# The sums of S: stored from SyncE's queue, one pair of slabs later, and no transfer on GpSimd's queue

## The chip, the cores and the metric

The kernel runs on one core of a Trainium2 chip. The metric is the device time of one execution in microseconds; lower is better. The times before are three executions of the same program. One further execution was profiled, and the profile page and all answers of the trace come from that one.

## The reference

Two layers of graph convolution on `x` of shape (8, 2048, 64), with one adjacency matrix `adj` of 2048 x 2048. Cut to what matters:

```python
# layer 0: each node has its own weights, mixed from 16 by an embedding
w = einsum('nd,dkio->nkio', embedding, weight)          # K = 3
A_stack = stack([I, A, 2*A@A - I])
x_g = einsum('knm,bmc->bnkc', A_stack, x)
x = layernorm(x + einsum('bnki,nkio->bno', x_g, w) + embedding @ bias)
# layer 1: diffusion convolution with the same matrix as both supports
x1 = A @ x0;  x2 = 2*A@x1 - x0
x = layernorm(x + concat([x0, x1, x2, x1, x2]) @ weight + bias)
```

So there are four multiplications by A: two hops in layer 0, two in layer 1. A is symmetric in its places of non-zero entries, and every row holds one value; the kernel uses A = diag(r) S, where S has ones and zeros, and checks this as it goes. Where it doesn't hold, a second, general program runs instead (a branch at the end of the first).

## The kernel before

**Stages.** The first hop (`hop_x`) multiplies S by x directly, in two passes g = 0 and 1, each over 16 slabs of A. The second hop uses seven products in place of eight (`seven_products`), which needs sums and differences of the quarters of S. Then comes layer 0's mix with the node weights (`mix0`), the third hop by seven products again, and the last hop directly.

**The first hop, where the change lies.** A step is one slab: k = kk + 8 j, for kk from 0 to 7 and j = 0, 1, so that two steps form a pair. A step loads 512 KB of A (`load_slab`, line 188) and, in pass 0, 256 KB of x. VectorE turns the slab into S (`places`, L200), ScalarE and VectorE split x into a high and a low half (L211, L215), and TensorE multiplies, 16 matmuls of 128x512 a step (L231). Once the second slab of a pair is there, `put_together` (lines 406 to 414) makes four sums or differences of quarters of S on VectorE (L413, four instructions), in bfloat16, into a piece of the buffer `z2` that is not in use yet, and stores the 512 KB into the DRAM tile `sums_of` (L414). ScalarE makes a bfloat16 copy of each slab and stores it too, 256 KB a pair, into `quarters` (L467). The seven products read both back through SyncE's queue (`load_sum`).

**What sets the order.** `run` (line 242) walks over the steps and calls each part of a step a given number of steps ahead: `operands`, with the loads and `put_together`, two steps before `use`, which holds the matmuls. `load` (line 117) and `ordered` keep the instructions of an engine in the order in which the code names them, so SyncE's queue issues its transfers in that order: for a step x, then the slab, then whatever `loads` still holds. Slabs go into a ring of five buffers (`RAW`), S into a ring of four.

**The join with the first product.** The steps of the first of the seven products follow in the same `run`; it uses slabs of A again (`slab`, 512 KB each, eight of them), and each of its `operands` also takes one of the waiting constants off `loads` (512 KB each for `w`, 1 MB for `rrow`). Because SyncE's queue may run ahead of the engines, these transfers are issued while the first hop still runs.

**GpSimd's queue** carries only the sixteen stores of L414. In the general program, which isn't run for these inputs, it carries the loads of constants and the sixteen stores of the result.

Of the kernel before, what the change touches and what calls it, by code (L numbers as in the profile page):

```python
# [18 lines left out]
B, N, C = 8, 2048, 64  # L19
NT = N // P  # L20
D = 16
# [16 lines left out]
def pattern(  # L38
# [22 lines left out]
    nc = tc.nc  # L61
# [46 lines left out]
    emb_sb = pack_sb[:, : NT * D].rearrange("p (t d) -> p t d", d=D)  # L108
    bias1 = pack_sb[:, NT * D :]
# [3 lines left out]
    w = [const.tile([P, D, C], F32, tag=f"w{k}", name=f"w{k}") for k in range(3)]  # L113
# [8 lines left out]
    def ordered(ins):  # L122
        if in_order:
            tc.keep_in_program_order(ins)
# [63 lines left out]
    def load_slab(src, shape):  # L188
        raw = rawp.tile(shape, F32, tag="raw", name="raw")
        load(nc.sync, raw, src)  # L190
        return raw
# [18 lines left out]
    def high(src, to):  # L210
        ordered(nc.scalar.copy(to[0], src))  # L211

    def low(src, to):

        ordered(nc.vector.tensor_tensor(to[1], src, to[0], ALU.subtract))  # L215
# [184 lines left out]
    sums_of = scratch.tile([KK, 2, P, 4, Q], BF16, tag="sums", name="sums_of")  # L400
    S1, S2, S4, S3 = range(4)

    quarters = scratch.tile([KK, P, 2, 2, Q], BF16, tag="quarters", name="quarters")
    couple = []

    def put_together(g, kk, x0, x1):
        to = z2[:, 2 * (kk % 8) : 2 * (kk % 8) + 2, :].rearrange("p t n -> p (t n)").bitcast(BF16)
        to = to.rearrange("p (i n) -> p i n", i=4)
        for i, (a, b, op) in enumerate((
            (x0[:, 1], x1[:, 1], ALU.add), (to[:, S1], x0[:, 0], ALU.subtract),  # L410
            (x1[:, 0], to[:, S2], ALU.subtract), (x0[:, 0], x0[:, 1], ALU.subtract),
        )):
            ordered(nc.vector.tensor_tensor(to[:, i], a, b, op))  # L413
        ordered(nc.gpsimd.dma_start(out=sums_of[kk, g], in_=to))  # L414

    def hop_x(g, kk, j):
        k = kk + KK * j

        def features(got):
            if g == 0 and k == 0:  # L420
                got["raws"] = [load_slab(adj[h, 0, :, :Q], [P, Q]) for h in range(2)]

        def operands(got):
            if g == 0 and k == 0:

                s = got["s"] = spool.tile([P, 2, Q], F32R, tag="s", name="s")
                hl = got["hl"] = [hpool.tile([P, B * C], F32R, tag="hl", name="hl") for _ in range(2)]
                high(z[0][0], hl)
                for h in range(2):
                    ordered(nc.vector.tensor_scalar(s[:, h], got["raws"][h], 0.0, None, ALU.not_equal))  # L430
                    if h == 0:
                        low(z[0][0], hl)
            else:
                if g == 0:
                    load(nc.sync, z[0][k], x[k].rearrange("n b c -> n (b c)"))
                raw = load_slab(adj[:, k, :, g * Q : (g + 1) * Q].rearrange("h m n -> m h n"), [P, 2, Q])
                got["s"] = places(raw)
                got["hl"] = halves(z[0][k])
                if g == 1 and len(loads) > 6:
                    load(nc.sync, *loads.pop(0))  # L440
            couple.append(got["s"])
            if j == 1:
                put_together(g, kk, *couple)
                couple.clear()

        def out(i):
            t = 4 * g + i if i < 4 else 4 * g + i + 4
            a, r = accs[i], rcol[:, t : t + 1]
            if i % 2:
                ordered(nc.vector.tensor_scalar_mul(z[1][t], a, r))  # L450
            else:
                ordered(nc.scalar.activation(z[1][t], a, AF.Copy, scale=r))

        def use(got):
            s, hl = got["s"], got["hl"]
            if kk == 0 and j == 0:
                accs[:] = banks(8)
            last = kk == KK - 1 and j == 1
            add_block(accs, s.rearrange("p h n -> p (h n)"), hl, kk == 0 and j == 0, last)
            if last:  # L460
                for i in range(8 if g == 0 else 4):
                    out(i)
            seen = xcpool.tile([P, 2, Q], BF16, tag="ln_xc", name="seen")
            i = g * NT + k
            ordered(nc.scalar.activation(seen, s, AF.Copy, accum_out=nonzero[:, i : i + 1]))
            if j == 1:
                ordered(nc.scalar.dma_start(out=quarters[kk, :, :, g, :], in_=seen))  # L467
            if last and g == 1:

                todo.extend(lambda i=i: out(i) for i in range(4, 8))  # L470

        return [(4, features), (2, operands), (0, use)]


# [378 lines left out]
def general(  # L853
# [10 lines left out]
    nc = tc.nc  # L864
# [16 lines left out]
    emb_sb = const.tile([P, NT, D], F32, tag="emb", name="emb_sb")  # L881
# [3 lines left out]
    w = [const.tile([P, D, C], F32, tag=f"w{k}", name=f"w{k}") for k in range(3)]  # L885

    v = const.tile([P, 3, C], F32, tag="v", name="v")
    bias1 = const.tile([P, C], F32, tag="bias1", name="bias1")

    def load_constants():  # L890
        nc.gpsimd.dma_start(out=emb_sb, in_=pack[:, : NT * D].rearrange("p (t d) -> p t d", d=D))
        b0_sb = work.tile([D, C], F32, tag="ln_xc", name="b0_sb")
        nc.gpsimd.dma_start(out=b0_sb, in_=bias[0:D, N // 4 :])
        for g in range(4):
            eT = work.tile([D, N // 4], F32, tag="acc", name=f"eT{g}")
            nc.gpsimd.dma_start(out=eT, in_=bias[32 * g : 32 * g + D, : N // 4])
            pb = ps_tp.tile([P, 4, C], F32, tag="tp", name=f"pb{g}")
            for j in range(4):
                nc.tensor.matmul(pb[:, j, :], lhsT=eT[:, j * P : (j + 1) * P], rhs=b0_sb, start=True, stop=True)
            nc.vector.tensor_copy(ebias[:, g * 4 : (g + 1) * 4, :], pb)  # L900
        for k in range(3):
            nc.gpsimd.dma_start(out=w[k].rearrange("p d o -> p (d o)"), in_=w0[k])

        wl = work.tile([P, 5, C], F32, tag="ln_sq", name="wl")
        nc.gpsimd.dma_start(
            out=wl, in_=pack[:, NT * D + C :].rearrange("p (k o) -> p k o", k=5)
        )
        w24 = work.tile([P, C], F32, tag="x2", name="w24")  # L910
        nc.vector.tensor_add(w24, wl[:, 2, :], wl[:, 4, :])
        nc.vector.tensor_sub(v[:, 0, :], wl[:, 0, :], w24)
        for h in range(2):
            q = slice(h * C, (h + 1) * C)
            nc.vector.tensor_add(v[q, 0, :], v[q, 0, :], ident[q, q])
        nc.vector.tensor_add(v[:, 1, :], wl[:, 1, :], wl[:, 3, :])
        nc.vector.tensor_scalar_mul(v[:, 2, :], w24, 2.0)
        nc.gpsimd.dma_start(out=bias1, in_=pack[:, NT * D : NT * D + C])


    blocks = {}
# [45 lines left out]
    def layernorm(src):  # L967


        def col(name):  # L970
            return work.tile([P, B], F32, tag=name, name=name)

        def wide(c):
            return c.unsqueeze(2).to_broadcast([P, B, C])

        s = col("ln_s")
        nc.vector.tensor_reduce(s, src, AX.X, ALU.add)
        nm = col("ln_nm")
        nc.vector.tensor_scalar_mul(nm, s, -1.0 / C)
        xc = work.tile([P, B, C], F32, tag="ln_xc", name="xc")  # L980
        nc.gpsimd.tensor_tensor(xc, src, wide(nm), ALU.add)
        sq = work.tile([P, B, C], F32, tag="ln_sq", name="sq")
        nc.scalar.activation(sq, xc, AF.Square)
        ss = col("ln_ss")
        nc.vector.tensor_reduce(ss, sq, AX.X, ALU.add)
        va = col("ln_v")
        nc.vector.tensor_scalar(va, ss, 1.0 / C, EPS, ALU.mult, ALU.add)
        sd = col("ln_sd")
        nc.scalar.activation(sd, va, AF.Sqrt)
        r0 = col("ln_r0")  # L990
        nc.vector.reciprocal(r0, sd)

        q = col("ln_q")
        nc.vector.tensor_mul(q, r0, r0)
        nc.vector.tensor_mul(q, q, va)
        nc.vector.tensor_scalar(q, q, -0.5, 1.5, ALU.mult, ALU.add)
        r = col("ln_r")
        nc.vector.tensor_mul(r, r0, q)
        nc.gpsimd.tensor_tensor(xc, xc, wide(r), ALU.mult)
        return xc  # L1000
# [107 lines left out]
    for i, t in enumerate(order):  # L1108
        ph = hop(t, lambda k: z[k][:, 1], ks)
        acc = work.tile([P, B, C], F32, tag="acc", name="acc")  # L1110
        nc.vector.tensor_tensor(acc, ph, z[t][:, 0], ALU.add)
        prefetch(order, i, 3)
        nc.gpsimd.dma_start(out=out[t], in_=layernorm(acc))


def gnn_kernel(tc, x, xT, adj, diag, rcols, bias, pack, w0, out):
# [55 lines left out]
```

## Time and profile before

| | |
|---|---|
| median of three runs | 828.28 us (827.91 to 828.9) |
| the profiled execution, device time | 828.66 us |
| its span, first to last instruction | 826.8 us |
| TensorE (PE) busy | 812.6 us, 98% |
| VectorE (DVE) busy | 594.7 us, 72% |
| ScalarE (ACT) busy | 275.3 us, 33% |
| GpSimd (POOL) busy | 111.9 us, 14% |
| granted TensorE clock | 0.997 |

```profile
PE   9999999999999999999999999999999999999995
DMA  9997885544200000000000001130154435565631
GB/s 329 376 386 244 287 315 174 155 143 148 69 3 12 15 13 15 14 14 14 14 14 14 30 13 38 39 103 27 43 150 152 141 128 150 167 181 165 212 120 42
```

These are three rows of the page's busy slices: the span is cut into 40 equal parts of 20.7 us, and a digit is the busy share in tenths. The first hop fills the first six slices, the seven products of the second hop the next five. The DMA engines are fullest in the first three.

```profile
q1 hardware_dynamic: 61616, 78.49, 29.5%
q10 hardware_dynamic: 6944, 8.66, 3.0%
q0 software_dynamic: 2304, 8.39, 2.8%
```

These are the DMA queues, with packets, MB and the share of sixteen engines' span: q1 is SyncE's, q10 ScalarE's and q0 GpSimd's, whose 8.39 MB are the sixteen stores of 512 KB.

```profile
raw<-in_adj SPq DMA_DIRECT2D x67, 512.0 KB, 4.7
sums_of<-z POOLq DMA_DIRECT2D x16, 512.0 KB, 6.3
quarters<-seen ACTq DMA_DIRECT2D x16, 256.0 KB, 6.2
z<-in_x SPq DMA_DIRECT2D x15, 256.0 KB, 8.1
```

These are transfers by who issues them, with their size and the median time in us from the issue to the landing.

### The profile page before, as it was taken

To read this page: it belongs to the slowest core of one execution; us is meant where nothing else is said; L and a number is where in the kernel's file an instruction comes from. 1 tells how busy PE (TensorE), PEld (TensorE's weight loads), DVE (VectorE), ACT (ScalarE), POOL (GpSimd) and SP (SyncE) were. 2 spreads that over 40 slices of the span, in tenths; PEclk is the share of its full clock that TensorE was granted. 3 is DMA by queue.
4 is the path that set the end of the run, shared out by engine and by line. 5 is a ranking of instruction groups with operands and counts; after the bars stand their busy time and mean duration, and the time that the engine had idled before them with its cause. 6 is when DMAs were issued, how large, how long until landed. Compare 5 with 4: busy or idle time off the path is not lost.

```text
span 826.8 us, 14470 instructions
## 1 busy us (share of the span) xinstructions
PE 812.6 (98%) x5614; PEld 725.2 (88%) x5614; DVE 594.7 (72%) x1303; ACT 275.3 (33%) x496; POOL 111.9 (14%) x121
## 2 busy tenths in 40 slices
PE   9999999999999999999999999999999999999995
PEld 6888888888788999999999999999878888888884
DVE  6878658763467888888888888888867546758762
ACT  5436445877401111111111101111287664203110
POOL 0000000000641111111110111111100000003341
PEclk9999999999999999999999999999999999999998
DMA  9997885544200000000000001130154435565631
GB/s 329 376 386 244 287 315 174 155 143 148 69 3 12 15 13 15 14 14 14 14 14 14 30 13 38 39 103 27 43 150 152 141 128 150 167 181 165 212 120 42
DMA packets 70940, 96.54 MB, mean 117 GB/s; under 512 B 4432, under 2 KB 45648, under 8 KB 70736
## 3 DMA queue, kind: packets, MB, share of 16 engines
q1 hardware_dynamic: 61616, 78.49, 29.5%
q10 hardware_dynamic: 6944, 8.66, 3.0%
q0 software_dynamic: 2304, 8.39, 2.8%
q8 instruction: 46, 0.75, 0.4%
q14 instruction: 30, 0.25, 0.1%
HBM read 78.75 MB, written 16.78 MB: 116 GB/s over the span
## 4 chain that ended last, share of the span: by engine, by line
PE 92%; issue 3%; DVE 3%; POOL 1%; ACT 1%; DVEq 0%; POOLq 0%; ACTq 0%
PE pm L361 36%; PE accT L558 24%; PE acc L231 14%; PE a L231 8%; PE accT L231 5%; PE pu L380 2%; DVE acc L367 2%; POOL z L609 1%; PE pt L274 1%; PE accT L662 1%; PE first L135 1%; POOL xc L322 0%; POOL got L337 0%; ACT sq L310 0%; DVE s L200 0%
## 5 line engine op out<-in xcount | busy, mean ns | idle before, releaser
L367 DVE SCALAR_TENSOR_TENSOR acc<-pm,pack_sb,acc 128x256 f32<-128x256 f32 x512 | 246.3, 483 | 41.6 <-PE pm L361 20.5
L558 PE MATMUL accT<-s,hl 128*128 128x512 f32 x896 | 205.6, 390 | 1.9 <-DVE s L200 1.4
L558 PEld LDWEIGHTS accT<-s,hl 128*128 128x128 f32 x896 | 167.6, 188 | 37.7 <-issue 1.8
L361 PE MATMUL pm<-w,xt 64*128 64x256 f32 x1024 | 160.9, 378 | 1.1 <-DVE acc L367 1.1
L361 PE MATMUL pm<-w,t 64*128 64x256 f32 x1024 | 160.0, 376 | 0.2 <-ACT t L276 0.2
L361 PE MATMUL pm<-w,z 64*128 64x256 f32 x1024 | 159.9, 376 | 0.0
L231 PE MATMUL acc<-hl,s 128*128 128x512 f32 x512 | 117.1, 390 | 0.0
L546 ACT CAST s<-raw 128x1024 fp32r<-128x1024 bf16 x96 | 101.0, 1052 | 40.2 <-ACT hl L211 32.2
L231 PEld LDWEIGHTS acc<-hl,s 128*128 128x128 f32 x512 | 95.8, 188 | 21.1 <-DVE hl L215 0.7
L361 PEld LDWEIGHTS pm<-w,t 64*128 64x128 f32 x1024 | 110.7, 187 | 1.9 <-ACT t L276 0.6
L361 PEld LDWEIGHTS pm<-w,z 64*128 64x128 f32 x1024 | 110.8, 187 | 1.4
L361 PEld LDWEIGHTS pm<-w,xt 64*128 64x128 f32 x1024 | 108.4, 187 | 2.5 <-issue 1.2
L276 ACT COPY hT<-pt 128x512 f32<-128x512 f32 x15 | 8.8, 587 | 197.4 <-PE pt L274 197.4
L231 PE MATMUL a<-hl,s 128*128 128x512 f32 x320 | 73.0, 389 | 0.0
L231 PEld LDWEIGHTS a<-hl,s 128*128 128x128 f32 x320 | 60.0, 188 | 12.5
L211 ACT CAST hl<-z 128x256 fp32r<-128x256 f32 (+1 forms) x96 | 47.1, 510 | 67.6 <-PE acc L231 36.4
L215 DVE TENSOR_TENSOR hl<-z,hl 128x512 fp32r<-128x512 f32 (+1 forms) x96 | 52.5, 552 | 21.2 <-ACT hl L211 18.4
L322 POOL TENSOR_TENSOR xc<-acc,s 128x512 f32<-128x512 f32 x16 | 16.7, 1043 | 279.5 <-DVE s L320 265.4
L200 DVE TENSOR_SCALAR s<-raw 128x1024 fp32r<-128x1024 f32 x47 | 33.2, 706 | 16.5 <-PE acc L231 10.9
L231 PE MATMUL accT<-hl,s 128*128 128x512 f32 x192 | 44.2, 390 | 0.0
L231 PEld LDWEIGHTS accT<-hl,s 128*128 128x128 f32 x192 | 35.9, 188 | 7.4
L347 POOL TENSOR_TENSOR acc<-z,ebias 128x256 f32<-128x256 f32 x32 | 22.7, 731 | 90.5 <-DVE hl L215 87.2
(105 smaller groups left out, 603.3 us busy)
## 6 DMA issues: line engine op xcount, KB each, us to landing
raw<-in_adj SPq DMA_DIRECT2D x67, 512.0 KB, 4.7
raw<-sums_of SPq DMA_DIRECT2D x64, 256.0 KB, 2.8
sums_of<-z POOLq DMA_DIRECT2D x16, 512.0 KB, 6.3
raw<-quarters SPq DMA_DIRECT2D x32, 256.0 KB, 2.6
raw<-in_adj SPq DMA_DIRECT2D x16, 384.0 KB, 3.5
quarters<-seen ACTq DMA_DIRECT2D x16, 256.0 KB, 6.2
xt<-in_xT SPq DMA_DIRECT2D x16, 256.0 KB, 2.6
out<-got ACTq DMA_DIRECT2D x16, 256.0 KB, 3.9
```

Source lines behind the costliest of these rows:

```text
L200: ordered(nc.vector.tensor_scalar(s, raw, 0.0, None, ALU.not_equal))
L211: ordered(nc.scalar.copy(to[0], src))
L215: ordered(nc.vector.tensor_tensor(to[1], src, to[0], ALU.subtract))
L231: nc.tensor.matmul(accs[i], lhsT=s[:, i * P : (i + 1) * P], rhs=hl[h], start=(first and h == 0), stop=(last and h == 1),)
L276: ordered(nc.scalar.copy(tt.rearrange("p j (h n) -> p h j n", h=2), pt[:, :, : B // 2 * C].rearrange("p h (j n) -> p h j n", n=C)))
L322: ordered(nc.gpsimd.tensor_tensor(xc, src, wide(s), ALU.subtract))
L347: nc.gpsimd.tensor_tensor(part.rearrange("p (j i) c -> p j i c", j=2), bc(0, t)[:, 4 * g : 4 * g + 4, :].rearrange("p (i j) c -> p j i c", ...
L361: nc.tensor.matmul(pm[:, j, i], lhsT=tt[k][q, 2 * g + i, :], rhs=w[k][q, ds, :], start=(k == 0), stop=(k == 2),)
L367: ordered(nc.vector.scalar_tensor_tensor(part, pm[:, :, :, d, :].rearrange("p j i c -> p (j i) c"), emb_sb[:, t, dd : dd + 1], part, ALU.m ...
L380: nc.tensor.matmul(pm[:, j, i * 3 * C : (i + 1) * 3 * C], lhsT=hT[q, 2 * g + i, :], rhs=v[q], start=True, stop=True,)
L546: ordered(nc.scalar.copy(s, got["raw"]))
L558: nc.tensor.matmul(acc[i][:, c], lhsT=hl[h][:, i * P : (i + 1) * P], rhs=S[:, c * 512 : (c + 1) * 512], start=(kk == 0 and h == 0), stop=( ...
```

## The change

The store of a pair's sums is no longer issued by GpSimd as soon as they are made. It is put on a short list, and SyncE issues it when the next pair's sums have been written down in the program, so behind the loads of that pair. The last one is issued in the last step's `use`. In the general program all transfers of GpSimd's queue go to ScalarE's.

```diff
     quarters = scratch.tile([KK, P, 2, 2, Q], BF16, tag="quarters", name="quarters")
-    couple = []
+    couple, stores = [], []
...
             ordered(nc.vector.tensor_tensor(to[:, i], a, b, op))
-        ordered(nc.gpsimd.dma_start(out=sums_of[kk, g], in_=to))
+
+        stores.append(lambda: load(nc.sync, sums_of[kk, g], to))
+        if len(stores) > 1:
+            stores.pop(0)()
...
             if last and g == 1:
+                stores.pop(0)()
...
     def load_constants():
-        nc.gpsimd.dma_start(out=emb_sb, in_=pack[:, : NT * D].rearrange("p (t d) -> p t d", d=D))
+        nc.scalar.dma_start(out=emb_sb, in_=pack[:, : NT * D].rearrange("p (t d) -> p t d", d=D))
...
         prefetch(order, i, 3)
-        nc.gpsimd.dma_start(out=out[t], in_=layernorm(acc))
+        nc.scalar.dma_start(out=out[t], in_=layernorm(acc))
```

The other transfers of `load_constants` in the general program are changed in the same way.

More of the change, by code (lines that the diff above doesn't have):

```diff
@@ L890, in load_constants @@
     def load_constants():
-        nc.gpsimd.dma_start(out=emb_sb, in_=pack[:, : NT * D].rearrange("p (t d) -> p t d", d=D))
+        nc.scalar.dma_start(out=emb_sb, in_=pack[:, : NT * D].rearrange("p (t d) -> p t d", d=D))
         b0_sb = work.tile([D, C], F32, tag="ln_xc", name="b0_sb")
-        nc.gpsimd.dma_start(out=b0_sb, in_=bias[0:D, N // 4 :])
+        nc.scalar.dma_start(out=b0_sb, in_=bias[0:D, N // 4 :])
         for g in range(4):
             eT = work.tile([D, N // 4], F32, tag="acc", name=f"eT{g}")
-            nc.gpsimd.dma_start(out=eT, in_=bias[32 * g : 32 * g + D, : N // 4])
+            nc.scalar.dma_start(out=eT, in_=bias[32 * g : 32 * g + D, : N // 4])
             pb = ps_tp.tile([P, 4, C], F32, tag="tp", name=f"pb{g}")
@@ L901, in load_constants @@
         for k in range(3):
-            nc.gpsimd.dma_start(out=w[k].rearrange("p d o -> p (d o)"), in_=w0[k])
+            nc.scalar.dma_start(out=w[k].rearrange("p d o -> p (d o)"), in_=w0[k])
         wl = work.tile([P, 5, C], F32, tag="ln_sq", name="wl")
-        nc.gpsimd.dma_start(
+        nc.scalar.dma_start(
             out=wl, in_=pack[:, NT * D + C :].rearrange("p (k o) -> p k o", k=5)
@@ L917, in load_constants @@
         nc.vector.tensor_scalar_mul(v[:, 2, :], w24, 2.0)
-        nc.gpsimd.dma_start(out=bias1, in_=pack[:, NT * D : NT * D + C])
+        nc.scalar.dma_start(out=bias1, in_=pack[:, NT * D : NT * D + C])
     blocks = {}
```

## The prediction

> **What bounds the kernel now.** I read the page first (PE busy 812.6 us of 826.8), then PE's waits over the span (two of about 1 us each in the whole middle), then a table of stretches over the two passes in which the sums of S are made and stored, because all sixteen transfers that move are issued between 12.9 and 116.0 us.
>
> ```profile
> core 0: us, PE busy (x) PEld busy (x) DVE busy (x) ACT busy (x) POOL busy (x), PEclk, DMA share, GB/s
> 0.00:20.00 20.00, 18.71 (x72) 12.79 (x73) 12.99 (x24) 10.89 (x18) 1.97 (x8) 1.00 0.92 327
> 20.00:40.00 20.00, 20.00 (x90) 16.57 (x89) 16.19 (x27) 9.22 (x17) 1.60 (x3) 1.00 1.02 374
> 40.00:60.00 20.00, 20.00 (x90) 16.55 (x89) 15.60 (x25) 8.13 (x15) 1.60 (x3) 1.00 1.04 393
> 100.00:120.00 20.00, 20.00 (x90) 16.57 (x89) 11.27 (x19) 7.49 (x15) 1.30 (x2) 1.00 0.88 298
> ```
>
> PE never stops, so there is nothing to win here from earlier or cheaper transfers. But the DMA engines are full as well (share 1.02 and 1.04, 374 and 393 GB/s), so a loss of feed can become a PE stall. The reader is to see both. PE takes 90 matmuls in 20 us, 0.222 us each; in stretches without a join it takes 37 in 8 us, 0.216 us. A step has 16, so 3.46 us, and a pair of slabs 6.9 us.
>
> Next, SyncE's waits up to 130 us. They say that it runs ahead until a raw buffer comes free or until an older transfer lands:
>
> ```profile
> SPq L118 <- DVE s L200: 60.9, 20, 8.2
> SPq L118 <- DMA raw<-in_adj: 13.0, 10, 3.6
> SPq L118 <- DMA z<-in_x: 9.4, 9, 1.8
> SPq L118 <- DMA quarters<-seen: 6.7, 3, 5.1
> ```
>
> The last row is ACT's transfer holding up SP. At 4.95 us SP issues after eight transfers of SP and ACT, just when the first of the eight has landed (ACT's cast of it starts at 4.96). I infer that SP and ACT together keep eight transfers in flight.
>
> **What the Trainium skill says.** "DMA: Bandwidth & Descriptors", section "Issuing engines are not separate DMA queues": all issuers end on the same 16 engines, and another issuer saves only issue time. The trace agrees: the share is full whatever the queue, and POOL's issue costs 0.56 us after 6.7 us of idle POOL on average (106.5 us over sixteen). Same page, "Queues, rings and completion order": an engine takes one ring in ring order and goes round robin between rings. So a store on SyncE's ring stands ahead of later loads instead of sharing with them; no run here separates the two yet. Same page, "Anatomy of one DMA — SWDGE (gpsimd) path": the semaphore waits for the receipt of the write, slow for HBM. Here sums_of takes 6.3 us to land (median of sixteen, 3.0 at the least), so such a slot is held long.
>
> **The change, part by part.**
>
> *POOL's sixteen issues go* (16 x 0.56 = 9.0 us). POOL has no other work in the two passes; nobody waits for it there. Worth 0. Bytes stay: 16 x 512 KB.
>
> *SP gets sixteen issues.* SP's own rows are 0.33 to 0.57 us; 16 x 0.45 = 7 us on a queue that waits over 90 us in this stretch. Issue time itself: 0. What matters is that SP now waits, in order, for VectorE's four subtractions of the pair before. Behind the store of pair p-1 stand the loads of pair p+1 (x twice, slab twice). Until now these were held by five raw buffers and the eight slots only.
>
> The tightest place is the start, in the timeline:
>
> ```profile
> 5.33 0.71 SPq L118 DMA_DIRECT2D raw<-in_adj  x1
> 6.75 0.50 SPq L118 DMA_DIRECT2D raw<-in_adj  x1
> 11.95 0.68 DVE L413 TENSOR_TENSOR z<-s 128x512 bf16<-128x512 f32 x1
> 12.94 0.73 POOL L414 DMA_DIRECT2D sums_of<-z  x1 [11.64 <-DVE z L413]
> 17.61 0.69 DVE L200 TENSOR_SCALAR s<-raw 128x1024 fp32r<-128x1024 f32 x1
> ```
>
> The store of pair 0 comes after slab 3 (issued 5.33) in the new order and needs the subtraction that ends at 11.95 + 0.68 = 12.6. So slab 4, issued at 6.75 now, is issued at about 13.5 (store 12.7, x 13.1). The 3.15 MB before it are moved by about 11.4 (per-microsecond stretches add to 3.0 MB by 11 us), so the DMA engines idle some 2.5 us. Then in ring order: bytes start 1.2 us after issue, 13.9 (nearest: the quickest 512 KB store takes 3.0 us to land, of which 1.35 is movement at 390 GB/s; of the 1.65 left I allow a little more, 1.2 ahead and 0.7 behind); store, quarters and x, 1.05 MB, to 16.6; slab 4 to 17.95; landed 0.7 later, 18.6. VectorE makes s and the low half by 20.0 (0.69 and 0.69, starts 0.6 apart). PE needs step 4 at 13.88 + 2 x 3.46 = 20.8. Cover left: 0.8 us, where it was 1.9. Both ends for this place: no loss, or with a restart 2 us slower, 1.2 us. I take 0. After it each pair asks 0.52 + 0.26 + 1.57 = 2.36 MB, 6.0 us at 390 GB/s, against PE's 6.9, so the lead grows by 0.9 a pair. The slots work against it: six transfers a pair in place of five, and a load may wait for a quarters store that landed 7.8 us after issue. By the same count step 8 has between 0.7 and 2.5 us left. Taken as 0; the bad end is 1 us. In the second pass no x is loaded, 1.84 MB or 4.7 us a pair: no loss.
>
> The second tight place is the join with the first product, whose slabs SP fetched early:
>
> ```profile
> 101.80 0.33 SPq L118 DMA_DIRECT2D raw<-in_adj  x1
> 105.66 0.33 SPq L118 DMA_DIRECT2D raw<-in_adj  x1
> 109.83 0.33 SPq L118 DMA_DIRECT2D raw<-in_adj  x1
> 115.05 0.68 DVE L413 TENSOR_TENSOR z<-s 128x512 bf16<-128x512 f32 x1
> 116.03 0.76 POOL L414 DMA_DIRECT2D sums_of<-z  x1 [10.18 <-DVE z L413]
> 116.70 0.33 SPq L118 DMA_DIRECT2D raw<-in_adj  x1
> 125.07 0.69 DVE L200 TENSOR_SCALAR s<-raw 128x1024 fp32r<-128x1024 f32 x1
> ```
>
> The last store is put behind the product's slabs 0 and 1 and needs 115.05 + 0.68 = 115.7. Its slabs 2, 3 and 4, issued at 101.8, 105.7 and 109.8 with a weight of 512 KB each, move behind it. From 117.2 at 390 GB/s the ring holds: store 1.35, then slab and weight three times (8.0), slab 5 (1.35), the row of 1 MB (2.7), a sum (0.7), slab 6 (1.35), with 0.7 for quarters between. Slab 2 lands at about 120.5 (needed 125.1), slab 5 at 129.3 (needed by PE at 132.8), slab 6 at 134 where it is issued at 125.8 as before. Slab 6 is then ready for PE at 134.7; PE's timeline has the product's step 4 at 131.03, a step of 8 matmuls is 1.73, so step 6 is asked for at 134.5. Slab 7 is about even. I take 0.4 us; bounds 0 (the ring runs at the 400 to 420 GB/s of 22 to 24 us) and 2 us (slots and receipts add a wait to each).
>
> *The end of the program*, two lists of queue events, of the closing line and of the branch:
>
> ```profile
> L1165 POOLq DRAIN  x3: 40/107/1372, 824.5 to 826.5; - x3
> L1165 SPq DRAIN  x3: 7/7/7, 825.2 to 826.2; - x3
> L1165 ACTq DRAIN  x2: 8/8/8, 825.1 to 826.2; - x2
> ```
> ```profile
> L1121 ACTq EVENT_SEMAPHORE  x1: 17/17/17, 825.0 to 825.0; - x1
> L1121 POOLq INC_SWDGE_SEM  x1: 512/512/512, 824.0 to 824.0; - x1
> ```
>
> The last barrier waits for POOL: an increment for the software queue (0.512 us from 824.0), then a drain of 1.372 us to 825.9. ACT and SP are there at 825.1 and 825.3. With no software transfer, in the skipped branch too (its twenty-seven issues move to ACT and never run), the increment has no object; POOL then comes 0.5 us or more earlier, and SP or ACT is next at about 825.3. Gain 0.6 us at most; if the increment stays, 0; if ACT must make up the skipped semaphores, some 0.02 us each, 0.2 less. I take 0.6. Outside the span lie 828.66 - 826.8 = 1.9 us, which no row prices; left as it is, bounds 1.2 us of gain and nothing lost, since fewer queues have nothing to add there.
>
> *Sum:* 828.66 - 0.6 + 0.4 = 828.46 for the profiled execution. That one stands 0.4 above the median of the runs, 828.28, so I put 828.1.
>
> **The rivals.** Forecast, 60%: covered transfers, a small loss at the join, a small gain at the end, in all within 0.2% (1.66 us, about what a measurement of this kernel can tell from no change): 827.0 to 829.8.
>
> Slower, 30%: SP's wait for VectorE stands ahead of the loads, and the feed of PE breaks. For it: DMA share over 1.0 in 20 to 60 us, 2.5 us of idle DMA at the start, 0.8 us of cover at step 4. Against it: 0.9 us regained per pair. It decides once slab 4 lands 0.8 us later than worked out. Price: 1.2 at step 4, 1 at step 8, 2 at the join, less 0.6: 3.6, so 828.28 + 3.6 = 831.9; at half of these, 830.3. If the slots held every pair of the first pass by 1 us, 8 us, 836; I give that 5 of the 30.
>
> Faster, 10%: no stall, and the unpriced 1.9 us outside the span shrink with the queue: 828.28 - 0.6 - 1.2 = 826.5. For it: only the software queue's events at the end. Against: no row there names that queue.
>
> That the stores stay on a software queue is excluded by the line itself; that the end doesn't shorten lies in the forecast (828.7).
>
> **Range and chances.** 826.9 to 832.0: it leaves out the 5% at 836 and the far ends of the other two, and takes in the bounds of the start, the join and the end. The forecast alone has 827.0 to 829.8. Faster 0.10, same 0.60, slower 0.30.
>
> **What would show it.** Right: no software queue in the list of queues and q1 at 87 MB; no increment at 824 and the last barrier 0.6 us earlier; the DMA share falling between 11 and 14 us; slab 4's VectorE pass at 18.6; still 90 matmuls in each 20 us from 20 to 120 us. Wrong: fewer than 88 in one of these, or PE waiting for L200 or L215 after 20 us; a PE gap over 1 us between 126 and 137 us; a change in later stages, where I have no mechanism at all.

## The result, and the profile after

The changed kernel takes 834.38 us (median of 6 runs, 833.47 to 835.09) against 828.45 us before: a ratio of 1.0073 with a 95% interval of 1.0063 to 1.0082, about 6 us slower. The profiled execution has 834.71 us and a span of 832.9.

First the table of stretches for the changed kernel (columns as before; the number after PE's busy time is its matmuls, the column after POOL the granted TensorE clock):

```profile
20.00:40.00 20.00, 20.00 (x89) 16.44 (x88) 15.07 (x24) 10.04 (x18) 0.00 (x0) 1.00 1.00 354
40.00:60.00 20.00, 20.00 (x90) 16.53 (x89) 14.44 (x23) 10.20 (x19) 0.00 (x0) 1.00 0.97 331
60.00:80.00 20.00, 16.91 (x67) 13.26 (x66) 17.65 (x29) 10.71 (x19) 0.00 (x0) 0.91 0.89 277
69.00:70.00 1.00, 1.00 (x3) 0.77 (x4) 1.00 (x2) 1.00 (x4) 0.00 (x0) 0.50 1.12 385
70.00:71.00 1.00, 1.00 (x4) 0.81 (x3) 1.00 (x3) 0.71 (x2) 0.00 (x0) 0.50 0.93 231
71.00:72.00 1.00, 1.00 (x3) 0.74 (x3) 1.00 (x3) 0.00 (x0) 0.00 (x0) 0.50 1.00 258
72.00:73.00 1.00, 1.00 (x5) 0.84 (x4) 1.00 (x2) 0.44 (x1) 0.00 (x0) 0.88 1.00 205
```

Inside the first pass nothing is lost that matters: 89 and 90 matmuls in 20 us. The loss is in 60 to 80 us, 67 matmuls in place of 89. That is the boundary between the two passes of the first hop. TensorE stands still for 3.1 us (it starts again at 68.21, below), and soon after the granted clock is 0.50 for about three microseconds.

What ends that standstill is in the timeline of the changed kernel (start, duration, engine, line, operation; in brackets the idle time ahead and what ended it):

```profile
58.10 0.38 SPq L118 DMA_DIRECT2D raw<-in_adj  x1
62.45 0.69 ACT L455 ACTIVATE z<-acc,rcol 128x512 f32<-128x512 f32 x1 [2.10 <-PE acc L231]
63.55 0.69 DVE L200 TENSOR_SCALAR s<-raw 128x1024 fp32r<-128x1024 f32 x1 [0.95 <-DMA raw<-in_adj]
66.81 0.68 DVE L413 TENSOR_TENSOR z<-s 128x512 bf16<-128x512 f32 x1
67.41 2.72 DVE L453 TENSOR_SCALAR z<-acc,rcol 128x512 f32<-128x512 f32 x4
68.21 12.06 PE L231 MATMUL acc<-hl,s 128*128 128x512 f32 x44 [3.09 <-DVE z L453]
```

At the end of a pass ScalarE and VectorE each evict four of the eight accumulators (lines 450 and 452 before, 453 and 455 now), and the next pass needs those banks. ScalarE begins at 62.45. VectorE's four stand in its queue behind its work on the second slab of the second pass, and that slab lands only at 63.5. VectorE then needs 3.9 us for it (S, the low half, four subtractions). So the evictions run from 67.41, and TensorE waits for them, not for a slab. Before, VectorE had made that slab's S at 57.5 us and its first eviction ran at 62.76, and TensorE ran through:

```profile
5.63 117.17 PE L231 MATMUL acc<-hl,s 128*128 128x512 f32 x512
57.50 0.69 DVE L200 TENSOR_SCALAR s<-raw 128x1024 fp32r<-128x1024 f32 x1 [2.10 <-PE acc L231]
62.76 0.75 DVE L450 TENSOR_SCALAR z<-acc,rcol 128x512 f32<-128x512 f32 x1 [1.30 <-ACT z L452]
```

The second loss is at the join. First the list of PE's waits (total, times, longest), then PE's timeline there:

```profile
PE acc L231 <- DVE z L453: 3.1, 1, 3.1
PE accT L562 <- DVE s L200: 2.3, 2, 1.4
```
```profile
143.68 89.13 PE L562 MATMUL accT<-s,hl 128*128 128x512 f32 x392 [0.97 <-DVE s L200]
```

The product's last slab reaches TensorE late: 0.97 us of the 2.3 lie here. The other wait of that list, 1.4 us, is no loss of the change, for the kernel before has it too; its row of the same list, and its timeline from the product's fifth slab on, without a gap:

```profile
PE accT L558 <- DVE s L200: 1.4, 1, 1.4
```
```profile
131.03 94.59 PE L558 MATMUL accT<-s,hl 128*128 128x512 f32 x416
```

The mix with the node weights begins at 232.75 us, where it began at 225.55: 7.2 us of loss up to there, 5.5 of them there already when the join begins (128.17 against 122.64). The end gives a part back. These are rows of two lists of queue events of the changed kernel, and then ScalarE's branch of the kernel before:

```profile
L1169 POOLq DRAIN  x3: 34/45/82, 830.5 to 832.7; - x3
```
```profile
L1125 ACTq COMPARE_BRANCH  x1: 58/58/58, 829.1 to 829.1; - x1
```
```profile
L1121 ACTq COMPARE_BRANCH  x1: 58/58/58, 822.1 to 822.1; - x1
```

The increment for the software queue is gone and POOL's long drain with it. From ScalarE's branch to the end of the span it is 3.8 us (832.9 - 829.1), where it was 4.7 (826.8 - 822.1): 0.9 us won.

### The profile page after: what moved, and what is told of

The parts are those of the page before. It is cut to its first block, busy times and chain, and to the rows that moved or that the text cites. A ratio compares the mean times of both kernels' runs of the same rounds, so it can differ in the third digit from the quotient of the medians.

```text
span 832.9 us, 14419 instructions
## 1 busy us (share of the span) xinstructions
PE 815.3 (98%) x5614; PEld 725.9 (87%) x5614; DVE 595.2 (71%) x1303; ACT 275.3 (33%) x496; POOL 103.0 (12%) x105
## 4 chain that ended last, share of the span: by engine, by line
PE 84%; DMA 8%; DVE 4%; issue 2%; ACT 1%; POOL 0%; SPq 0%; DVEq 0%; POOLq 0%; ACTq 0%
PE pm L361 38%; PE accT L562 22%; PE a L231 8%; PE acc L231 7%; PE accT L231 5%; DMA quarters<-seen 4%; PE pu L380 2%; DMA raw<-in_adj 2%; DMA z<-in_x 2%; DVE acc L367 2%; PE pt L274 1%; PE accT L666 1%; DVE z L413 1%; ACT seen L468 1%; DVE s L200 0%
## 5 line engine op out<-in xcount | busy, mean ns | idle before, releaser
L231 PE MATMUL acc<-hl,s 128*128 128x512 f32 x512 | 119.3, 394 | 3.7 <-DVE z L453 3.1
```

Of the source, the lines that this page charges most:

```text
L231: nc.tensor.matmul(accs[i], lhsT=s[:, i * P : (i + 1) * P], rhs=hl[h], start=(first and h == 0), stop=(last and h == 1),)
```

## The experiments

All times are medians beside runs of the kernel before on the same chip (828.45 us for the first four, 828.37 for the others).

**Evictions ahead of the late slab.** VectorE's and ScalarE's preparation of the second slab of pass 1 is held until the evictions have been named; its load keeps its place. (`prepare` holds what stood there: S, the two halves and the sums.)

```diff
+                if (g, kk, j) == (1, 0, 1):
+                    held.append(lambda: prepare(got, raw))
+                    return
...
                 for i in range(8 if g == 0 else 4):
                     out(i)
+                if g == 0:
+                    held.pop(0)()
```

> The changed kernel, with VectorE's four evictions at the end of the first pass named ahead of its work on the second slab of the second pass. Theory 1 (the late slab costs only because VectorE's evictions stand behind it, and TensorE waits for the banks they free): the 5 us lost at the boundary of the passes go, the loss of 1.7 us at the join stays: 829 to 830 us against 834.4. Rival (the feed is late in itself, and TensorE would next wait for that slab): at most 1 us faster, 833.4 or more.

Measured: 828.98 us, ratio 1.0007 (0.9998 to 1.0015), at the lower edge of theory 1. Its timeline and its stretch at the boundary:

```profile
63.01 0.75 DVE L461 TENSOR_SCALAR z<-acc,rcol 128x512 f32<-128x512 f32 x1 [1.80 <-ACT z L463]
66.39 0.68 DVE L200 TENSOR_SCALAR s<-raw 128x1024 fp32r<-128x1024 f32 x1
```
```profile
60.00:80.00 20.00, 20.00 (x89) 16.39 (x89) 16.39 (x27) 13.20 (x24) 0.00 (x0) 1.00 0.76 253
```

VectorE evicts at 63.01 and turns to the slab afterwards; 89 matmuls are back, at full clock. 5.4 us are won by the order of work on VectorE, and of one cast on ScalarE, with the same transfers in the same order on SyncE. The feed of TensorE was not too thin; theory 1 holds, and the low clock went with the standstill.

**Quarters from GpSimd's queue.** Why was the slab late? It was issued at 58.10, after 2.9 us in which SyncE waited for a quarters store to land; the chain of waits names that transfer. (A slot is one of the eight transfers that the prediction took SyncE and ScalarE to keep in flight together.)

```diff
-                ordered(nc.scalar.dma_start(out=quarters[kk, :, :, g, :], in_=seen))
+                ordered(nc.gpsimd.dma_start(out=quarters[kk, :, :, g, :], in_=seen))
```

> The changed kernel, with the quarters stored from GpSimd's queue in place of ScalarE's; the sums stay on SyncE's, one pair later. Theory 2 (slots: SyncE's load of the second slab waits until a quarters store of ScalarE has landed, because the two queues share eight slots): the wait is gone, the slab is issued near 54.5 us in place of 58.1, and both stalls go; the software queue's events at the end come back: 828 to 829 us. Rival (order: SyncE stands behind VectorE's subtractions whatever the slots): 833 or more.

Measured: 834.18 us (4 runs), as its rival has it. From its timeline:

```profile
55.31 0.43 SPq L118 DMA_DIRECT2D raw<-in_adj  x1
63.57 0.69 DVE L200 TENSOR_SCALAR s<-raw 128x1024 fp32r<-128x1024 f32 x1 [1.46 <-DMA raw<-in_adj]
68.23 6.05 PE L231 MATMUL acc<-hl,s 128*128 128x512 f32 x19 [3.33 <-DVE z L453]
```

The wait for quarters is gone and the slab is issued 2.8 us earlier, but it lands at the same time, 8.2 us after its issue. The likely reason is what SyncE had issued within the 2.2 us before it, a store, a slab and the bias, 1.3 MB in all; no run tests that by itself. The chain's wait for a slot was true and not the cause.

**Stores two pairs later.**

```diff
-        if len(stores) > 1:
+        if len(stores) > 2:
...
-                stores.pop(0)()
+                while stores:
+                    stores.pop(0)()
```

> The changed kernel, with each store two pairs later in place of one. Rival, order (SyncE is held by the wait for the subtractions of the pair before): SyncE never waits for VectorE's sums any more, both stalls go, 827 to 828.5 us. Theory 2, slots: a quarters store still holds up the slab at the boundary, 832 us or more. Between 829 and 832 both have a part.

Measured: 829.16 us, ratio 1.0007 (0.9998 to 1.0016). The first rows of its list of SyncE's waits up to 135 us, and the hop in PE's timeline:

```profile
SPq L118 <- DVE z L413: 37.2, 12, 5.5
SPq L118 <- DMA quarters<-seen: 20.7, 7, 6.7
```
```profile
6.09 117.02 PE L231 MATMUL acc<-hl,s 128*128 128x512 f32 x512
```

SyncE waits 37.2 us for the subtractions where the changed kernel has 65.9, and more than twice as long for quarters (20.7 against 9.0), and the hop runs through in 117.0 us as before. So it is SyncE's wait for VectorE that makes the slab late. The first stall goes; the one at the join stays (PE is idle for 0.97 us before 138.18). With it the time lies just above 829, where its expectation gives both theories a part; the waits for slots, which have grown, cost nothing at the boundary, and the experiments on the constants below take up the join.

**Stores from ScalarE's queue, one pair later.**

```diff
-        stores.append(lambda: load(nc.sync, sums_of[kk, g], to))
+        stores.append(lambda: load(nc.scalar, sums_of[kk, g], to))
```

> The changed kernel, with the sums stored from ScalarE's queue, one pair later, in place of SyncE's. SyncE then issues loads alone and waits for no subtraction; the slots taken are the same in number. Order: both stalls go, 827 to 828.5 us. Slots: the waits of SyncE for quarters and sums stores stay, 832 us or more.

Measured: 828.92 us, ratio 1.0006 (0.9997 to 1.0014). Neither stall is left, with six transfers a pair as in the changed kernel: a second result against the slots. It missed the 828.5 named for it. PE's timeline shows one reason: the matmuls of the node bias stand in two groups, 1.1 us each, where one of 1.1 us stood before. Why the two take twice as long isn't shown.

```profile
126.22 1.11 PE L146 MATMUL accT<-bias_sb 16*128 16x64 f32 x16
...
131.11 1.11 PE L146 MATMUL accT<-bias_sb 16*128 16x64 f32 x16
```

**The two halves of the change alone.** First the general program's part alone, on the kernel before (the stores stay on GpSimd's queue).

> The kernel before, with the general program's transfers moved to ScalarE's queue and nothing else: the sums stay on GpSimd's queue. Theory 3 (the 0.9 us won at the end of the program come from the skipped branch alone, which no longer has to make up for software transfers): 827.3 to 827.8 us against 828.45. Rival (the software queue in use at all is what costs at the end): 828.2 to 828.7.

Measured: 828.22 us, ratio 0.9999 (0.9990 to 1.0007), as the rival has it. Then the stores alone, with the general program left on GpSimd's queue.

> The change without its part in the general program: the stores move, the general program keeps GpSimd's queue. Theory 3: the end is longer by 0.9 us again, 835.0 to 835.6 against 834.4. Rival: as the changed kernel, 834 to 834.6.

Measured: 835.43 us (4 runs, 832.78 to 836.55), inside the range of theory 3, but not for its reason. The queue events at the end, by the lists of the closing line and of the branch. Of the part in the general program:

```profile
L1165 POOLq DRAIN  x3: 44/107/1374, 823.2 to 825.5; - x3
```
```profile
L1121 ACTq COMPARE_BRANCH  x1: 58/58/58, 821.9 to 821.9; - x1
```

And of the stores alone:

```profile
L1169 POOLq DRAIN  x3: 34/45/93, 831.8 to 833.3; - x3
```
```profile
L1125 ACTq COMPARE_BRANCH  x1: 58/58/58, 829.7 to 829.7; - x1
L1125 POOLq INC_SWDGE_SEM  x1: 168/168/168, 831.6 to 831.6; - x1
```

In the first the increment is gone and the drain of 1.374 us starts earlier, beside other waits; in the second the increment is there and the drain is short. Both take 3.8 to 3.9 us from the branch to the end (spans of 825.7 and 833.6 us). So theory 3 falls as it was put. By these traces, one of each kernel, increment and drain reach past the other engines only together, and either half of the change is enough to hide them. Nor did the first half win time that can be measured: its median span is 0.6 us shorter (826.0 against 826.6), but 2.19 us lie outside the span in place of 1.82. What makes those 0.37 us stays open. That the stores alone are 1 us slower than the whole change isn't settled: their four runs lie up to 3.8 us apart, and the one profiled stood still for 4.0 us at the boundary in place of 3.1.

**Constants beside the second product**, on top of the evictions ahead.

```diff
-                if loads:
+                if loads and p > 0:
                     load(nc.sync, *loads.pop(0))
```

> The changed kernel, with the evictions ahead as in the first experiment, and the six constants loaded beside the second product in place of the first. Theory 4 (the loss at the join is bytes: 4 MB of constants stand between the last store and the first product's slabs 6 and 7): the gap of 1.2 us before the first product's last step goes, and with it 1.5 us or so: 827.2 to 827.8 us against 829.0 of the first experiment. Rival (a slot held by the last quarters store, or the last store itself): 828.6 or more.

Measured: 827.63 us, ratio 0.9992 (0.9984 to 1.0001). Its join in PE's timeline:

```profile
130.72 11.63 PE L572 MATMUL accT<-s,hl 128*128 128x512 f32 x50
```

No gap, where the first experiment has one:

```profile
138.23 89.14 PE L572 MATMUL accT<-s,hl 128*128 128x512 f32 x392 [1.21 <-DVE s L200]
```

1.35 us are won on the first experiment. That alone doesn't separate bytes from slots, since six transfers left the queue together with their bytes, and in the changed kernel SyncE waits 4.1 us for the last quarters store before it issues the product's last slab. The run with quarters from GpSimd's queue does. These are the issue of that slab in the changed kernel, then its issue and TensorE's gap in that run:

```profile
137.40 0.33 SPq L118 DMA_DIRECT2D raw<-in_adj  x1
```
```profile
132.81 0.33 SPq L118 DMA_DIRECT2D raw<-in_adj  x1
143.42 89.13 PE L562 MATMUL accT<-s,hl 128*128 128x512 f32 x392 [1.32 <-DVE s L200]
```

Issued 4.6 us earlier, it still keeps TensorE waiting until the same time. So the slot isn't what costs here either, and the loss goes with the constants ahead of the slabs, as theory 4 has it. Their amount is 2.5 MB, three weights of 512 KB and the row of 1 MB, and not the 4 that the expectation names.

**The same, two pairs later.**

> As the one before, with the stores two pairs later. If the wait of SyncE for the subtractions still costs anything anywhere, this is faster than it by 0.3 us or more; otherwise the same, 827.2 to 827.8 us.

Measured: 827.34 us over 21 runs, ratio 0.9988 (0.9981 to 0.9995). Beside 827.63 the 0.3 is at the edge of what was named, too little to settle whether SyncE's wait still costs anything. This kernel is 1.0 us faster than the kernel before and 7.0 faster than the changed one.

## Why the prediction was wrong

*That TensorE bounds the first hop and POOL's issues are worth nothing*: right, as far as the runs show. No version won time in the hop beyond the scatter of the profiles (116.5 us in the profile of the general program's part alone, which doesn't touch the hop, 117.2 in the kernel before).

*The start*: right in kind. The store went out at 12.96, slab 4 at 13.82 (13.5 worked out), VectorE took it up at 20.19 and not 18.6; moved bytes fell to 254 GB/s over the first 20 us from 327. The cover of 0.8 us was used up, at little cost: the weight loads wait 0.22 us for that slab at 21.54. The first pass ends 0.4 us later (ScalarE's first eviction at 62.45, before at 62.03), and a wait of 0.37 us at 9.83, ahead of the first store, is likely part of that.

*"The lead grows by 0.9 a pair"*: this is the first step that failed, and it made the slab late. It set bytes against time, 6.0 us of transfer against 6.9 of TensorE, as if the queue were always full. But SyncE could issue a pair's loads only after the subtractions of two pairs before, and those waited for the slabs issued a round ago. That ring (subtractions, issue, transfer, subtractions) has its own length. VectorE's low halves of the first slab of every second pair show it in the changed kernel:

```profile
20.80 0.68 DVE L215 TENSOR_TENSOR hl<-z,hl 128x512 fp32r<-128x512 f32 x1
34.59 0.68 DVE L215 TENSOR_TENSOR hl<-z,hl 128x512 fp32r<-128x512 f32 x1
47.55 0.68 DVE L215 TENSOR_TENSOR hl<-z,hl 128x512 fp32r<-128x512 f32 x1
61.91 0.68 DVE L215 TENSOR_TENSOR hl<-z,hl 128x512 fp32r<-128x512 f32 x1
```

They start 13.0 to 14.4 us apart for two pairs, about as long as TensorE's 13.9. So the lead hardly grew, and the DMA engines moved 331 to 354 GB/s where they had moved 374 to 393.

*"In the second pass no x is loaded: no loss"*: this is the step that cost the time. It is true of the transfers, and the place of the loss all the same. The prediction named SyncE's queue behind the new wait, the loads, and then asked only when TensorE needs the slabs. It didn't ask what stands behind VectorE's wait for a slab. There stand the four evictions which TensorE needs at the boundary. That term was 0 in the sum and measured 5.4 us (834.38 - 828.98): a standstill of 3.1 us and then the half clock. The late slab by itself costs next to nothing: in the first experiment it was issued 1.6 us earlier (56.54), VectorE turned to it only at 66.39, and TensorE never stood still. The sign named for a wrong forecast, fewer than 88 matmuls in a stretch of 20 us, came with 67.

*The join*: right in kind, the product's last slab is late behind the constants. It was the last of the eight, which the forecast had about even, and not the one before. This term was mis-sized: 0.4 us worked out, 1.35 measured by moving the constants.

*The end*: the increment vanished and the barrier came earlier, 0.9 us in the span where 0.6 was worked out; the drain's fall from 1.372 to 0.08 us wasn't foreseen.

*The rivals*: the slower one was right in its first half, SyncE's wait standing ahead of the loads, and not in its second: in the hop the feed of TensorE didn't break. Its price, 3.6 us at the start, step 8 and the join, was put in the wrong places, and the variant of 1 us lost in each pair didn't come. That its 831.9 lies nearest to the result is in part luck.

*Slips in the working*: half of the slower rival's 3.6 us makes 830.1 and not 830.3, and SyncE's rows are not all within 0.33 to 0.57 us, since one that the prediction shows has 0.71. Neither bears on the result.

## What to carry to other kernels

When a change makes a transfer late, look at the queue of each engine that waits for its data, not only at the consumer in the end: an eviction or a release that happens to stand behind the wait can be what the bound engine needs next. A rate of bytes says little about a queue that waits, in order, for a result of its own loads; count the length of that ring. And where a late input can't be avoided, try naming the work that frees buffers ahead of it: here that was worth 5.4 us and cost nothing that shows.

## What was not expected of the hardware

After the standstill at 65.1 to 68.2 us the granted TensorE clock was 0.91, then 0.50 for three microseconds and 0.88 in the next, with 3 to 4 matmuls a microsecond in place of 6. In the experiment with the evictions ahead, which has no standstill, it stayed at 1.00. A stall of 3.1 us was thus followed by a loss of more than a microsecond (of 22 matmuls lost at 0.222 us, 4.9 us, the stall is 3.1); after the gap of 1 us at the join the granted clock stayed at 1.00.
